# W's first two chunks in halves, proj's first part ahead of them on the same queue, a constant for the constant passes, and m_0's first j copied alone

## The chip, the cores and the metric

The kernel runs on one core of a Trainium2 chip. Its time is the device time of one execution in microseconds (us). Before the change the median of three executions is 317.30 us (317.02 to 317.35).

A core has a matrix engine (TensorE, in the profile PE, with its weight loads as PEld), a vector engine (DVE), a scalar engine (ACT), GpSimd (POOL), and a sync engine (SP) that issues most transfers here. Every engine takes its instructions in order and waits on semaphores for the others. SP, ACT and POOL each have a queue of transfers; all queues are served by the same 16 DMA engines.

## What is computed

Eight sequences x of 512 tokens by 2048 features pass through a conditioning layer with a LoRA adapter per sequence, then through a feed-forward of eight low-rank experts of which each token takes one, and the result is added to x. Cut to what matters:

```python
# conditioning: W (2048 x 2048), one adapter (A, Bm) of rank 16 per sequence
y = einsum('bti,oi->bto', x, W) + b
y = y + einsum('btr,bro->bto', einsum('bti,bir->btr', x, A), Bm) * 2.0
# experts: 8 of rank 16, the best one per token
logits = einsum('bsd,ed->bse', y, route_w)
route_weight = one_hot(argmax(logits)) * max(logits)
h  = einsum('bsd,erd->bser', y, A_ffn)
out = einsum('bser,eor->bso', route_weight[..., None] * h, Bw)
return x + out
```

Everything is float32.

## The kernel before

y is never built. Its only use is a projection on 136 columns: 8 experts x 16 ranks and 8 router rows, side by side in `proj` (2048 x 136). So the kernel folds first: c = W^T proj, a 2048 x 136 matrix, and for each sequence b a matrix m_b = c + the adapter's part. Then each tile of 128 tokens needs only x m_b (the "heads"), the choice of an expert, and one product with `fb`, the experts' second factors (the "deltas"), which is added to x.

**Stage 1, folding (0 to about 70 us).** W comes in 16 chunks of 128 output rows, `w_0` to `w_15`, each a tile of 128 x 2048 (1 MB), six buffers in turn (`load_w`, L104). `pj` is proj as a tile of 128 x 16 x 136, loaded in parts: `load_pj(c0, c1)` (L99) brings the parts c0 to c1 - 1. For chunk oc, `fold_w` (L286) makes 16 matmuls, one for each j (128 of W's columns): the stationary operand is `w_oc[:, j]`, the moving one `pj[:, oc]` of 136 columns, and the result adds up in PSUM over all 16 chunks. A float32 matmul takes two passes of PE, each a weight load and a pass. The results of the 16 j lie in six PSUM banks: `bank_js` (L210) puts j 0 to 2 in bank 0, 4 to 6 in bank 1, 8 to 10 in bank 2, 12 to 14 in bank 3, 3 and 7 in bank 4, 11 and 15 in bank 5, and `fold_w` goes through the banks in the order 0, 1, 4, 2, 3, 5. So its first eight matmuls are j 0 to 7, which read the first 1024 columns of the chunk.

`chunk_w(oc)` (L272) stands ahead of each chunk. It lets ACT and DVE copy one element per partition of the chunk into `paced`, so that both wait until the chunk has landed, and then has SP issue the chunk four further on.

**The start.** The order in the program is: DVE fills `warm`, a 128 x 128 tile, with ones. ACT issues pj's part 0. SP issues w_0, w_1, pj's parts 3 and 4, w_2, pj's parts 5 to 7, w_3. ACT makes one small copy (which loads its function table) and then issues pj's parts 1 and 2. PE multiplies `warm` by `warm` 11 times (22 passes, L136) into a PSUM tile that nobody reads, and then waits for w_0 and pj's part 0. `warm` is used once more, much later, in `project_bias` (L320).

**The end of stage 1.** After the last chunk, ACT copies the six banks to SBUF as c (L299), and `first_products` (L356) adds the adapter's part of sequence 0 to the same banks: 16 small matmuls, j by j over the banks. Then the six banks are copied to SBUF as m_0, alternately by DVE (banks 0, 2, 4) and ACT (banks 1, 3, 5) (L367). `place` finds where a bank's j lie in m_0.

**Stage 2, tokens (about 71.5 us to the end).** 32 tiles of 128 tokens. `heads(t, ...)` (L478) multiplies the transposed tile xT_t with m_b: 16 matmuls (j 0 to 15, in this order), in two halves. DVE routes, PE multiplies with `fb` (`delta`, L628), DVE adds to x (`add_delta`, L650), SP stores. ACT and POOL move 32-row blocks of x into `xq` and DVE transposes them into xT (`shuffle`, `turn_x`). The order of all this is written out by hand; nothing is reordered by a scheduler. x comes in units of two tiles through five buffers, of which the last two take memory that W's tiles and pj gave up.

**Transfers and their counters.** A transfer issued by SP or ACT signals its landing on one of eight counters, taken in turn over the program. An issue that takes a counter whose former transfer is not known to have landed waits for that.

Of the kernel before, what the change touches and what calls it, by code (L numbers as in the profile page):

```python
# [18 lines left out]
def kernel(  # L19
# [32 lines left out]
    nc = tc.nc  # L52
    P = 128
    Q = 32
    NQ = P // Q
    B, T, D = x.shape
# [32 lines left out]
    warm = const.tile([P, P], F32, name="warm")  # L89
# [9 lines left out]
    def load_pj(c0, c1, eng=nc.sync):  # L99
        eng.dma_start(out=pj[:, c0:c1, :], in_=proj_v[:, c0:c1, :])  # L100

    w_tiles = []

    def load_w(oc):  # L104
        wt = wpool.tile([P, D], F32, tag="w", bufs=6, name=f"w_{oc}")
        nc.sync.dma_start(out=wt, in_=w[ts(oc, P), :])
        w_tiles.append(wt)

    load_pj(0, 1, nc.scalar)
    load_w(0)  # L110
    load_w(1)
    load_pj(3, 5)
    load_w(2)
    load_pj(5, 8)
    load_w(3)
# [14 lines left out]
    make_identity(nc, ident)  # L130

    nc.scalar.copy(warm_a[:, 1:2], warm_a[:, :1])
    load_pj(1, 3, nc.scalar)
    pm = ps_s.tile([P, P], F32, tag="s", name="pm")
    for _ in range(11):
        nc.tensor.matmul(pm, warm, warm, start=True, stop=True)  # L136

    own_i = const.tile([P, B], I32, name="own_i")
    nc.gpsimd.iota(own_i, pattern=[[-R, B]], base=0, channel_multiplier=1)
# [62 lines left out]
    parts = (JC, NJ - JC)  # L202

    def at(j):
        q, n = divmod(j, NQ)
        return (1, q) if n == 3 else (0, 3 * q + n)
# [3 lines left out]
    bank_js = {}  # L210
# [5 lines left out]
    ms = {0: [const.tile([P, n, NP], F32, name=f"m0_{n}") for n in parts]}  # L216
# [51 lines left out]
    pcs = [ps_c.tile([P, GRP, NP], F32, name=f"pc_{z}") for z in range(len(bank_js))]  # L268

    paced = const.tile([P, 2], F32, name="paced")  # L270

    def chunk_w(oc):  # L272


        nc.scalar.copy(paced[:, :1], w_tiles[oc][:, :1])  # L275
        nc.vector.tensor_copy(paced[:, 1:], w_tiles[oc][:, :1])  # L276
        if oc + 4 < NO:
            if oc in (2, 3):
                load_pj(4 * oc, 4 * oc + 4)
            load_w(oc + 4)  # L280

    def place(m, js):
        part, n = at(js[0])
        return m[part][:, ds(n, len(js)), :]
# [60 lines left out]
    def adapter_product(b, out, q, n, start=True):  # L345
        nc.tensor.matmul(  # L346
            out,
            ad_q[ts(q, Q), b // 2, n, :],
            g4[ts(q, Q), b, :],
            start=start,  # L350
            stop=True,
            skip_group_check=not start,
            tile_position=(q * Q, 0),
        )

    def first_products():  # L356


        for n in range(3):
            for q in range(NQ):  # L360
                adapter_product(0, pcs[q][:, n, :], q, n, start=False)
        for n in range(2):
            for k in range(2):
                adapter_product(0, pcs[NQ + k][:, n, :], k * HQ, 3 + n, start=False)
        for z in range(NQ + 2):
            js = bank_js[z]
            (nc.scalar.copy if z % 2 else nc.vector.tensor_copy)(  # L367
                place(ms[0], js), pcs[z][:, : len(js), :]
            )

    chunk_w(0)
    for oc in range(NO):
        if oc + 1 < NO:
            chunk_w(oc + 1)
# [42 lines left out]
        if oc == 14:  # L417
            for h in range(2):
                turn_x(0, h)
    first_products()  # L420
    wctx.close()
    ps_o = ctx.enter_context(tc.tile_pool(name="ps_o", bufs=2, space=bass.MemoryType.PSUM))
# [275 lines left out]
    for n in range(2 * NT + LAG + 1):  # L698
# [31 lines left out]
        for q, r in due.get(n - 2, ()):  # L730
            u, k = divmod(q, TPU)
# [50 lines left out]
```

## Time and profile before

The profiled execution took 316.97 us; its span, from the first instruction to the last, is 315.2 us, so 1.8 us lie around it.

| | before |
|---|---|
| median of three executions | 317.30 us (317.02 to 317.35) |
| profiled execution, and its span | 316.97 us, 315.2 us |
| constant passes (L136): first, count, ns of one | 1.06 us, 22, 421 |
| real passes of the folding (L290): first, count, ns of one | 6.38 us, 512, 279 |
| transfer of w_0, w_1, w_2: landing (issue) | 6.15 (0.75), 8.9 (1.2), 12.1 (2.1) us |
| pj's part 0, parts 1 and 2 (ACT's queue): landing (issue) | 6.34 (0.75), 9.35 (1.25) us |
| m_0 copies: ACT, DVE | 70.86 to 72.05, 70.89 to 72.31 us |
| heads: first pass | 71.53 us |

How to read it: a row of the timeline gives the start of a group of instructions in us from the span's start, its length, the engine (SPq and ACTq are the issuing of transfers on SP and ACT), the line of the kernel, the operation, the tile written and the tile read, how many, and in square brackets how long the engine was idle before it and what released it. The chain of waits follows the work that ended last back to the start, at each step to what released it. [...]passes overlap: what counts for the time is the distance from start to start.

### The profile page before, as it was taken

How to read it: one execution, taken by the hardware profiler on the slowest of the kernel's cores; microseconds unless marked ns; L12 is line 12 of the kernel's file. 1: busy time of each engine (PE TensorE's matmuls, PEld its weight loads, DVE VectorE, ACT ScalarE, POOL GpSimd, SP SyncE). 2: the span in 40 equal slices, each digit the busy share in tenths (PEclk: the TensorE clock that was granted, in tenths of full speed). 3: DMA queues.
4: the chain of work that ended last, by engine and by line, in shares of the span. 5: the costliest groups of instructions: out<-in, count | busy, mean ns of one | idle time of the engine just before them, and what ended most of it. 6: DMA issues, size and time to landing. Idle time of an engine off the chain costs nothing.

```text
span 315.2 us, 5653 instructions
## 1 busy us (share of the span) xinstructions
PE 309.1 (98%) x2114; PEld 245.0 (78%) x2114; DVE 230.2 (73%) x390; ACT 189.5 (60%) x311; POOL 187.4 (59%) x284
## 2 busy tenths in 40 slices
PE   8999999999999999999999999999999999999994
PEld 7999999999777877777777768677767777777741
DVE  1010595937999798677988787888788887979684
ACT  2000133738799399559949983998499669912110
POOL 1011083979997866429884975698388929722220
PEclk9999999999999999999999999999999999999998
DMA  7999999989333957784877694848676876253467
GB/s 282 408 361 413 420 419 420 418 338 390 147 135 133 312 222 250 286 286 199 297 289 298 244 384 181 361 164 372 224 309 257 337 295 247 100 234 134 164 243 261
DMA packets 15595, 88.52 MB, mean 281 GB/s; under 512 B 1728, under 2 KB 4048, under 8 KB 5456
## 3 DMA queue, kind: packets, MB, share of 16 engines
q1 hardware_dynamic: 14400, 85.45, 68.9%
q0 software_dynamic: 320, 2.11, 1.6%
q10 hardware_dynamic: 848, 0.61, 0.6%
q8 instruction: 16, 0.26, 0.3%
q14 instruction: 11, 0.09, 0.1%
HBM read 54.60 MB, written 33.55 MB: 280 GB/s over the span
## 4 chain that ended last, share of the span: by engine, by line
PE 96%; DMA 2%; DVE 1%; DVEq 0%; issue 0%
PE ph L482 38%; PE po L648 33%; PE pc L290 19%; DMA pj<-in_proj_dram 2%; PE po L346 2%; PE pg L330 1%; PE ph L648 1%; PE ph L346 1%; PE pe_o L648 1%; DVE x L654 0%; PE pc L346 0%; PE pw L592 0%; DVE m L367 0%; DVEq L778 0%; PE pb L322 0%
## 5 line engine op out<-in xcount | busy, mean ns | idle before, releaser
L253 ACT COPY xq<-x 32x1024 f32<-32x1024 f32 x135 | 140.8, 1043 | 9.6 <-DMA x<-in_x_dram 4.8
L482 PEld LDWEIGHTS ph<-m,xT 128*128 128x128 f32 x1024 | 126.6, 190 | 25.4 <-issue 20.1
L253 POOL COPY xq<-x 32x1024 f32<-32x1024 f32 x121 | 125.5, 1037 | 22.8 <-DMA x<-in_x_dram 6.6
L482 PE MATMUL ph<-m,xT 128*128 128x136 f32 x1024 | 129.7, 280 | 0.3 <-DVE m L367 0.3
L648 PE MATMUL po<-fb,whT 128*128 128x512 f32 x240 | 111.8, 592 | 0.0
L654 DVE TENSOR_TENSOR x<-x,po 128x1024 f32<-128x1024 f32 x60 | 72.5, 1209 | 24.1 <-PE po L648 23.5
L237 DVE STREAM_TRANSPOSE xT<-xq 128x1024 f32<-128x1024 f32 x64 | 78.8, 1235 | 3.8 <-POOL xq L253 3.0
L648 PEld LDWEIGHTS po<-fb,whT 128*128 128x128 f32 x240 | 41.6, 190 | 31.6 <-issue 30.9
L290 PE MATMUL pc<-pj,w 128*128 128x136 f32 x512 | 59.9, 279 | 0.3 <-DMA pj<-in_proj_dram 0.3
L290 PEld LDWEIGHTS pc<-pj,w 128*128 128x128 f32 x512 | 59.5, 190 | 0.6 <-DMA pj<-in_proj_dram 0.6
L610 POOL COPY wq<-wh 32x64 f32<-32x64 f32 (+1 forms) x117 | 26.4, 226 | 54.0 <-DVE wh L534 40.9
L610 ACT COPY wq<-wh 32x64 f32<-32x64 f32 (+1 forms) x91 | 21.6, 238 | 21.3 <-DVE wh L503 10.0
L275 ACT COPY paced<-w 128x1 f32<-128x1 f32 x16 | 3.1, 191 | 39.7 <-DMA w<-in_w_dram 39.7
L276 DVE COPY paced<-w 128x1 f32<-128x1 f32 x16 | 2.4, 151 | 30.7 <-DMA w<-in_w_dram 30.6
L567 ACT COPY m<-ph 128x136 f32<-128x136 f32 x24 | 4.9, 284 | 26.7 <-PE ph L346 22.6
L578 POOL TENSOR_TENSOR m<-m,c 128x408 f32<-128x408 f32 x14 | 14.4, 1052 | 1.6 <-ACT m L573 1.1
L224 POOL COPY ad_q<-ad_ar 32x512 f32<-32x512 f32 x12 | 8.0, 668 | 10.0 <-DMA ad_ar<-in_cond_a_dram,arow_i 9.5
L388 POOL DMA_DIRECT2D bias_o<-in_bias_dram x1 | 0.7, 737 | 17.9 <-DVE bias_o L387 17.9
L571 DVE TENSOR_TENSOR m<-c,po 128x408 f32<-128x408 f32 x14 | 7.5, 576 | 4.0 <-PE po L346 3.9
L579 POOL TENSOR_TENSOR m<-m,c 128x544 f32<-128x544 f32 x7 | 9.4, 1343 | 0.0
L338 DVE TENSOR_TENSOR g<-pg,half 32x272 f32<-32x272 f32 x16 | 7.0, 437 | 3.2 <-PE pg L330 2.9
L615 DVE STREAM_TRANSPOSE whT<-wq 128x256 f32<-128x256 f32 (+1 forms) x13 | 5.2, 404 | 2.7 <-ACT wq L610 2.7
(81 smaller groups left out, 144.4 us busy)
## 6 DMA issues: line engine op xcount, KB each, us to landing
x<-in_x_dram SPq DMA_DIRECT2D x32, 1024.0 KB, 7.9
out_dram<-x SPq DMA_DIRECT2D x28, 1024.0 KB, 4.3
w<-in_w_dram SPq DMA_DIRECT2D x16, 1024.0 KB, 14.3
out_dram<-x SPq DMA_DIRECT2D x4, 512.0 KB, 2.6
out_dram<-x SPq DMA_DIRECT2D x6, 256.0 KB, 3.1
fb<-in_ffn_b_dram SPq DMA_DIRECT2D x1, 1024.0 KB, 17.5
pj<-in_proj_dram SPq DMA_DIRECT2D x2, 272.0 KB, 13.2
out_dram<-x ACTq DMA_DIRECT2D x1, 256.0 KB
```

The lines of the kernel that those rows point to most:

```text
L224: copy(dst[:, :NQ], src[:, ts(q, NQ)])
L237: nc.vector.transpose(dst[:, ts(h, HJ), :].rearrange("p j (g t) -> p g j t", t=Q), src.rearrange("p g (j a) -> p g j a", a=Q)[:, :, ts(h, ...
L253: copy(xq_tiles[u][ts(i, Q), :, g, :].rearrange("p k (j a) -> p k j a", a=Q), src[:, :, :, i, :],)
L290: nc.tensor.matmul(pcs[z][:, n, :], w_tiles[oc][:, ts(j, P)], pj[:, oc, :], start=(oc == 0 and n == 0), stop=(oc == NO - 1), skip_group_ch ...
L346: nc.tensor.matmul(out, ad_q[ts(q, Q), b // 2, n, :], g4[ts(q, Q), b, :], start=start, stop=True, skip_group_check=not start, tile_positio ...
L482: nc.tensor.matmul(ph, xT_tiles[t][:, j, :], place(m, (j,))[:, 0, :], start=(j == 0), stop=(j == NJ - 1),)
L571: nc.vector.tensor_tensor(place(m, js), place(cs, js), banks[q], ALU.add)
L578: nc.gpsimd.tensor_tensor(place(m, js), place(m, js), place(cs, js), ALU.add)
L579: nc.gpsimd.tensor_tensor(m[1], m[1], cs[1], ALU.add)
L610: copy(wq[ts(i, Q), :, ts(q, Q)], wh[ts(q, Q), :, ts(i, Q)])
L648: nc.tensor.matmul(part, whT_tiles[t], fb[:, cols], start=True, stop=True)
L654: nc.vector.tensor_tensor(xs, xs, part, ALU.add)
```

## The change

- `load_w` can bring a chunk in several transfers; w_0 and w_1 come in two of 1024 columns each, into the same tile.
- pj's part 0 is issued by SP, ahead of w_0, and not by ACT.
- ACT issues pj's parts 1 and 2 as two transfers.
- The 11 matmuls ahead of the first chunk read `ones`, a view of the one-column constant 1.0 that the framework writes before the kernel starts, repeated over 128 columns; not `warm`.
- `chunk_w` reads the last column of the chunk in the place of the first.
- m_0 is copied in seven pieces, not six: DVE takes j 0, ACT takes j 1 and 2 of bank 0, and then DVE bank 1, ACT bank 2, DVE bank 3, ACT bank 4, DVE bank 5.

```diff
-    def load_w(oc):
+    def load_w(oc, parts=1):
         wt = wpool.tile([P, D], F32, tag="w", bufs=6, name=f"w_{oc}")
-        nc.sync.dma_start(out=wt, in_=w[ts(oc, P), :])
+        for k in range(parts):
+            cols = ts(k, D // parts)
+            nc.sync.dma_start(out=wt[:, cols], in_=w[ts(oc, P), cols])
         w_tiles.append(wt)
 
-    load_pj(0, 1, nc.scalar)
-    load_w(0)
-    load_w(1)
+
+    load_pj(0, 1)
+    load_w(0, 2)
+    load_w(1, 2)
     load_pj(3, 5)
     load_w(2)
     load_pj(5, 8)
...
     nc.scalar.copy(warm_a[:, 1:2], warm_a[:, :1])
-    load_pj(1, 3, nc.scalar)
+    load_pj(1, 2, nc.scalar)
+    load_pj(2, 3, nc.scalar)
+    ones = nc.const_aps.tensor(1.0, [P, P])
     pm = ps_s.tile([P, P], F32, tag="s", name="pm")
     for _ in range(11):
-        nc.tensor.matmul(pm, warm, warm, start=True, stop=True)
+        nc.tensor.matmul(pm, ones, ones, start=True, stop=True)
...
-        nc.scalar.copy(paced[:, :1], w_tiles[oc][:, :1])
-        nc.vector.tensor_copy(paced[:, 1:], w_tiles[oc][:, :1])
+        nc.scalar.copy(paced[:, :1], w_tiles[oc][:, D - 1 :])
+        nc.vector.tensor_copy(paced[:, 1:], w_tiles[oc][:, D - 1 :])
...
-        for z in range(NQ + 2):
-            js = bank_js[z]
-            (nc.scalar.copy if z % 2 else nc.vector.tensor_copy)(
-                place(ms[0], js), pcs[z][:, : len(js), :]
-            )
+
+        copies = (nc.vector.tensor_copy, nc.scalar.copy)
+        cuts = ((0, 0, 1), (0, 1, 2), *((z, 0, len(bank_js[z])) for z in range(1, NQ + 2)))
+        for k, (z, n0, n) in enumerate(cuts):
+            js = bank_js[z][n0 : n0 + n]
+            copies[k % 2](place(ms[0], js), pcs[z][:, ds(n0, n), :])
```

## The prediction

> **What bounds the kernel now.** I read the page's busy shares first, then the chain that ended last, then the first 20 us of the timeline and the stretch around 71 us, where the chain leaves TensorE.
>
> ```profile
> PE 309.1 (98%) x2114; PEld 245.0 (78%) x2114; DVE 230.2 (73%) x390; ACT 189.5 (60%) x311; POOL 187.4 (59%) x284
> ```
>
> TensorE (PE) works 309.1 of 315.2 us, so an edit pays only where PE does not work, or works on nothing useful. The list of what PE waited for has three entries: 1.1 us for `warm` at the start, 0.3 us for `pj` at 6.38 us, 0.3 us for m_0 at 71.5 us. The change touches all three. The chain of waits, cut to its first 20 us:
>
> ```profile
> 0.75 5.59 DMA pj<-in_proj_dram
> 6.34 0.04 issue
> 6.38 13.70 PE pc L290 x116
> ```
>
> The chain begins with proj's first part: 5.59 us from issue to landing for 68 KB. From 6.38 us PE works without a break. The timeline of the same stretch shows what else stood there (start, length, engine and line):
>
> ```profile
> 0.75 0.41 ACTq L100 DMA_DIRECT2D pj<-in_proj_dram  x1
> 0.75 0.86 SPq L106 DMA_DIRECT2D w<-in_w_dram  x2
> 0.85 0.17 DVE L90 MEMSET warm<- 128x128 f32 x1 [0.85 <-PEq L767]
> 1.06 5.06 PE L136 MATMUL pm<-warm 128*128 128x128 f32 x22 [1.06 <-DVE warm_a L92]
> 6.19 0.19 ACT L275 COPY paced<-w 128x1 f32<-128x1 f32 x1 [3.52 <-DMA w<-in_w_dram]
> 8.99 0.19 ACT L275 COPY paced<-w 128x1 f32<-128x1 f32 x1 [2.61 <-DMA w<-in_w_dram]
> 12.17 0.19 ACT L275 COPY paced<-w 128x1 f32<-128x1 f32 x1 [2.98 <-DMA w<-in_w_dram]
> ```
>
> Three things end within 0.3 us of each other: the 22 constant passes (6.12), w_0 (6.15, seen by its `paced` copy at 6.19) and pj's first part (6.34). Moving one gains little; the change moves all three. What then ends last decides.
>
> **Part 1, constant passes.** They lose their wait for the memset of `warm` (0.85 to 1.02 us) and read a constant that POOL writes at 0.28 us, before the start barrier. SP and ACT issue at 0.75, DVE's first instruction runs at 0.85; I put PE's first pass at 0.85, 0.21 before its 1.06 (ends: 0.75 to 1.06). All 22 passes last 421 ns (the first 579) and start 0.213 us apart: (5.70 - 1.06 - 0.158) / 21. A real pass with 136 columns lasts 279 ns and starts 0.116 us after the last (44.75 us for 384 in the chain). So the constant passes run at half the rate per column, and the first real one at 6.38 at the full rate; the granted-clock row reads 1.00 throughout and does not show this switch. PE could take a real pass 0.213 us after the last constant pass started: 5.91 now, **5.70** changed.
>
> **Part 2, W and proj.** SP now issues pj (68 KB) first, then w_0 in two halves. One issue takes 0.41 to 0.43 us in the timeline, so w_0's first half is issued at 1.18, not 0.75. In the DMA view cut to 0 to 7 us the first bytes move at 1.8 us; about 0.21 MB have moved by 3.0, and from there 400 GB/s. w_0 and pj together (1.12 MB) have then moved at 3.0 + 0.91/0.40 = 5.3; w_0 lands at 6.15, so 0.87 us lie between last byte and landing. Changed, what must move until w_0's first half is in: pj 0.07, the half 0.52, and up to 0.07 of the proj part that ACT now issues beside it: 0.66 MB, at 3.0 + 0.45/0.40 = 4.1, plus 0.3 for the later issue, plus 0.87 = **5.3 us** (4.9 without the later issue; 5.75 with all of it and 4 KB rows a tenth slower and a slower start). pj, first in its queue, lands well before. So the passes end last, at 5.70, and the first real pass comes 6.38 - 5.70 = 0.68 us earlier.
>
> Here a rule of the Trainium skill speaks against the change: *DMA: Bandwidth & Descriptors*, "Rules for kernel authors", wants 128 partitions and at least 1 MiB per DMA, because (section "Anatomy of one DMA", a fit for the GpSimd path) each pays about 2.0 us besides bytes/436 GB/s. Paid one after the other, an estimate from that page makes 3.2 us of each half, and w_0 whole only at 1.18 + 6.4 = 7.6, with w_1 whole at 14.0. The rows deny that such costs add in a filled queue: w_1 landed 2.8 us after w_0, with 136 KB of pj between, which is 1.19 MB at 0.42 MB/us. I take the rows; the fixed part is paid once.
>
> What is late next? One chunk is 32 passes, 3.73 us. The second half of w_0 is read from 5.70 + 16 x 0.116 = 7.6; it lands near 6.7. Chunk 1 starts at 9.43: w_1 landed at 8.95 and lands perhaps 0.4 later whole, but only its first half (near 8.0) is asked for, and pj's part 1 is now a transfer of its own of 68 KB instead of 136 KB that landed at 9.35. Chunk 2 starts at 13.16; w_2 landed at 12.13, with 0.4 it is 12.5. Chunk 3 starts at 16.9, w_3 landed at 15.2. Later chunks have 2 us and more (w_8 34.1 against 36.2). `chunk_w` reads the last column, so ACT's and DVE's pacing copies wait for the whole tile as before; behind them stand only small works that nothing needs before chunk 12. Two more transfers on SP also shift the eight DMA counters: w_2's issue now waits for pj's first part to land (about 3.5), the parts 5 to 7 of pj for w_0's first half, w_3 for pj's part 1 (under 7). The queue holds bytes until about 10.6 at that time, so no engine runs dry; I cost these waits at nothing, and if w_3's issue came only at 11 its landing at 15.2 would slip towards its need at 16.9. At W's end the earlier start is kept: xT_0 is ready at 67.5 for heads at 71.5, g4 at 62.3 for 69.8, xT_2's first half at 79.8 for 81.2. After that loads follow stores, and PE hides both. At most 1.4 us pass through.
>
> **Part 3, first j of m_0.** The timeline around 71 us:
>
> ```profile
> 70.86 1.19 ACT L367 COPY m<-pc 128x408 f32<-128x408 f32 x3 [0.54 <-PE pc L346]
> 70.89 1.42 DVE L367 COPY m<-pc 128x408 f32<-128x408 f32 x3 [3.42 <-PE pc L346]
> 71.53 6.90 PE L482 MATMUL ph<-m,xT 128*128 128x136 f32 x56 [0.27 <-DVE m L367]
> ```
>
> ```profile
>   DVE m L367: 0.7, 2
> ```
>
> The last line is from the heads' line (L482) alone, 71.4 to 76 us: idle before it, in us, and how often. There are two waits for m, not one: 71.53 for j 0, and, pass by pass, a gap from 72.2 to 72.37 for j 3, which lies in bank 4, DVE's third copy (to 72.31). Changed, DVE copies j 0 alone: 0.28 us (ACT needs 273 to 278 ns for such a tile at L567, DVE 300 at L323), done at 71.18, and j 0 starts at 71.23, 0.3 earlier. But in the built order ACT's copy of j 1 and 2 waits for DVE's copy, since both read one bank; so ACT starts at 71.22, not 70.86, and does 272, 408 and 272 columns: 403 + 499 + 403 ns less two overlaps of 0.108 = 1.09, to **72.31**. Bank 4 is now ACT's last. j 3 starts at 72.37 either way: the gain goes into the second wait. I cost part 3 at 0 (ends -0.1 and +0.1 us). DVE and ACT are free 0.2 to 0.3 us later; xT_1 is then ready at 73.6 for its need at 75.4.
>
> **The sum, and the clock.** PE's early real passes may still be slow. *TensorE: Matmul & The Clock Gate* (Part 1) says the array runs at half clock until a busy window of about 3.4 us has passed, and that the window runs free of the kernel's start. The trace agrees as to size (half rate for at least 4.9 us, full rate at 6.38), and puts this execution's switch between 5.91 and 6.38. By the row: passes from 5.70 to the switch cost half that stretch, 0.10 to 0.34, so 0.68 - 0.22 = **0.46 us** is gained. By the rule the switch falls anywhere from 4.5 to 7.9: a late one leaves 0.34, an early one shortens the constant passes too, and then the data at 5.3 sets the start (up to 1.1). I take the row for the middle, the rule for the range. Profiled execution: 316.97 (span 315.2 and 1.8 around it) - 0.46 + 0 = **316.5 us**. The median shown, 317.30, lies 0.33 above that execution; whether the clock's switch makes that spread no run here shows.
>
> **Rivals.**
> *A. Early switch* (0.25): the passes end before 5.5 and W's half decides; 0.75 to 1.2 gained, 316.0. For it: the page's free window. Against: this execution switched late.
> *B. The half lands late* (0.12): at 6.2 instead of 5.3, because the start of the queue is slow (94 to 240 GB/s until 2.8 us); under 0.2 gained, 316.8 to 317.0.
> *C. Slower, by chunk 2* (0.08): 4 KB rows move slower than 8 KB rows, w_2 lands after 13.16 and PE stands. Price: w_0 and w_1 are 2.1 MB, 5.1 us at 410 GB/s; w_2 at 12.5 has 0.66 to spare, so loss begins at 13% slower, and it outweighs the 0.68 from 26% on. At 40% it would be 317.7. No load of 4 KB rows is in this trace; stores with such rows landed in 2.6 us, which tells little of a filled queue.
> *D. The constant does not do it* (0.05): a read that stays on one column is slower than 0.213 us a pass. From 14% on nothing is left; at twice, the start is at 10.4 and the time 321.
> The forecast has 0.50, with its own span 316.2 to 316.7.
>
> **Numbers.** 0.2% is 0.63 us, about what a measurement tells from none. The bound of faster lies that far below the median of before it is timed against: 316.67 by the one shown, 316.35 if that median came out like the profiled execution. Of the forecast's 0.50 I count 0.31 below it; with A's 0.24 that makes 0.55 faster; the rest of the forecast, B and the mild end of C make 0.35; slower keeps 0.10. The range 316.0 to 317.2 holds the forecast, most of A and B.
>
> **What would show it.** First constant pass near 0.85; first real pass at 5.6 to 5.8 with nothing between; some of the first real passes 0.23 apart; `paced` for w_0 after the first real pass; ph's first pass about 0.3 after j 0's product and a longer gap before the seventh; 98% PE as now. Wrong: a gap after the constant passes (B), a gap at chunk 2 or 3 (C), passes over 0.22 apart (D), or ph without its second gap.

## The result, and the profile after

The change makes the kernel slower: 317.82 us in the median of 17 executions (316.96 to 319.34) against 316.93 for the kernel before, timed beside it (316.60 to 317.35, 17 executions). The ratio is 1.0036, 95% interval 1.0025 to 1.0047 (here and below it is not the ratio of the two medians, which would be 1.0028). The forecast was 316.5 us, with a range of 316.0 to 317.2. The spread also grew, from 0.75 to 2.4 us.

| | before | after |
|---|---|---|
| profiled execution, and its span | 316.97, 315.2 us | 317.52, 315.8 us |
| constant passes: first, end | 1.06, 6.12 us | 0.79, 4.81 us |
| first real pass | 6.38 us | 6.44 us |
| w_0, w_1, w_2 landed whole (by ACT's pacing copy) | 6.19, 8.99, 12.17 us | 8.18, 10.83, 13.77 us |
| moved by the DMA engines, 3.0 to 6.5 us | 1.46 MB | 0.90 MB |
| heads: first pass | 71.53 us | 71.27 us |
| GpSimd's first copy of x_1 | 66.75 us | 67.66 us |
| t 3: first heads pass on the chain | 87.85 us | 88.52 us |

The chain of waits after the change, its first 20 us (start, length, what):

```profile
0.75 0.38 SPq L100
1.13 0.06 issue
1.19 5.11 DMA w<-in_w_dram
6.31 0.14 issue
6.44 13.56 PE pc L295 x115
```

The chain begins with SP's issue of proj's part 0 and goes on with w_0's first half, issued behind it: 5.11 us from issue to landing for half the bytes that took 5.4 us whole. The timeline of the stretch:

```profile
0.75 0.38 SPq L100 DMA_DIRECT2D pj<-in_proj_dram  x1
0.79 4.02 PE L141 MATMUL pm<-const-float32-1.0 128*128 128x128 f32 x22 [0.79 <-PEq L773]
1.19 2.03 SPq L108 DMA_DIRECT2D w<-in_w_dram  x4
6.44 13.79 PE L295 MATMUL pc<-pj,w 128*128 128x136 f32 x117 [1.63 <-DMA w<-in_w_dram]
8.18 0.19 ACT L280 COPY paced<-w 128x1 f32<-128x1 f32 x1 [5.94 <-DMA w<-in_w_dram]
10.83 0.19 ACT L280 COPY paced<-w 128x1 f32<-128x1 f32 x1 [2.46 <-DMA w<-in_w_dram]
13.77 0.19 ACT L280 COPY paced<-w 128x1 f32<-128x1 f32 x1 [2.75 <-DMA w<-in_w_dram]
```

The constant passes begin where they should. They end at 4.81, because in this execution the clock switched early, near 3.5 us (passes of 421 ns before, of 273 ns from there on). PE then stands 1.63 us: the bracket of the first real pass names W. The start is 0.06 us later than before. W's first eight chunks land 1.6 to 2.0 us later, the others 0.8 to 1.1 us.

Yet the adapter's products behind the folding begin where they began before (69.85 against 69.83). The 0.6 us are lost later. The chain from 78 to 91 us was PE alone before the change, with these two pieces at the place in question:

```profile
87.16 0.69 PE po L346 x24
87.85 2.05 PE ph L482 x16
```

After the change:

```profile
79.48 2.37 DVE xT L242 x2
...
84.03 1.21 DVE x L660
85.24 1.16 DVE xT L242
86.39 1.12 DVE x L660
87.51 0.04 issue
87.56 0.96 PE po L351 x20
88.52 2.05 PE ph L488 x16
```

Read it from the bottom: the heads of tile 3 come 0.67 us later than before, because `fold_adapter` (L351) needs PSUM that DVE's add (L660) frees; DVE is late since xT_2 is late; and xT_2 waited for GpSimd, which had waited for x_1. GpSimd's copies of x_1, before and after:

```profile
66.75 23.70 POOL L253 COPY xq<-x 32x1024 f32<-32x1024 f32 x22 [1.69 <-DMA x<-in_x_dram]
67.66 23.65 POOL L258 COPY xq<-x 32x1024 f32<-32x1024 f32 x22 [1.87 <-DMA x<-in_x_dram]
```

From there to xT_2 it is 11.85 us before and 11.82 after, so x_1's lateness passes through whole. The chain itself takes another way back, over a short wait of GpSimd at 74.83 us to DVE's m_0 copies (L375, 71.62); taken alone it would accuse those (theory M below).

From 8 to 63 us the page's row has the DMA engines at 90% or more and at about 410 GB/s on average, both times. That bytes not moved in the first 6.5 us therefore arrive later all the way down to x_1 is argued here; the experiments show how far it holds.

### The profile page after: what moved, and what is told of

It is laid out like the page before. It is cut to its first block, busy times and chain, and to the rows that moved or that the text cites. A ratio compares the mean times of both kernels' runs of the same rounds, so it can differ in the third digit from the quotient of the medians.

```text
span 315.8 us, 5660 instructions
## 1 busy us (share of the span) xinstructions
PE 308.8 (98%) x2114; PEld 244.4 (77%) x2114; DVE 230.2 (73%) x391; ACT 189.4 (60%) x311; POOL 186.9 (59%) x284
## 2 busy tenths in 40 slices
DMA packets 15899, 88.52 MB, mean 280 GB/s; under 512 B 1776, under 2 KB 4096, under 8 KB 6016
## 4 chain that ended last, share of the span: by engine, by line
PE 91%; DVE 4%; DMA 2%; POOL 1%; issue 0%; SPq 0%; DVEq 0%; POOLq 0%
PE ph L488 34%; PE po L654 32%; PE pc L295 19%; DVE xT L242 2%; PE po L351 2%; DMA w<-in_w_dram 2%; POOL xq L258 1%; PE pg L335 1%; PE ph L654 1%; DVE x L660 1%; PE ph L351 1%; PE pe_o L654 1%; DVE m L375 0%; PE pc L351 0%; DVE rw L507 0%
## 5 line engine op out<-in xcount | busy, mean ns | idle before, releaser
L258 ACT COPY xq<-x 32x1024 f32<-32x1024 f32 x135 | 140.8, 1043 | 10.9 <-DMA x<-in_x_dram 6.9
L660 DVE TENSOR_TENSOR x<-x,po 128x1024 f32<-128x1024 f32 x60 | 72.5, 1209 | 24.1 <-PE po L654 23.7
```

What stands on the lines that cost most here:

```text
L258: copy(xq_tiles[u][ts(i, Q), :, g, :].rearrange("p k (j a) -> p k j a", a=Q), src[:, :, :, i, :],)
L660: nc.vector.tensor_tensor(xs, xs, part, ALU.add)
```

## The experiments

Each was timed beside the kernel before, whose median was 316.78 to 316.84 us in all of them. **T** is the theory that the new transfers make the queue's start slower and that this is paid at x_1; **M** that the seven copies of m_0 are at fault. Where two kernels were not timed together, their ratios to the kernel before are compared.

### Which part: transfers, or the rest

e1 keeps only the transfers and the pacing column of the change; e2 keeps only the constant and the m_0 copies:

```diff
 e1, against after
-        nc.tensor.matmul(pm, ones, ones, start=True, stop=True)
+        nc.tensor.matmul(pm, warm, warm, start=True, stop=True)
...
 e2, against after
-    load_pj(0, 1)
-    load_w(0, 2)
-    load_w(1, 2)
+    load_pj(0, 1, nc.scalar)
+    load_w(0)
+    load_w(1)
...
-    load_pj(1, 2, nc.scalar)
-    load_pj(2, 3, nc.scalar)
+    load_pj(1, 3, nc.scalar)
```

> Only the transfers' part of the change: w_0 and w_1 in halves, proj's part 0 first on SP, parts 1 and 2 apart on ACT, pacing by the last column; constant passes and m_0 copies as before. Theory T (the queue's start moves fewer bytes, all of W and then x_1 land later, and DVE reaches its add before fold_adapter too late): slower than before by as much as the whole change, 0.5 to 1.3 us, x_1's first xq copy on GpSimd at 67.3 us or later (before 66.75), first real pass at 6.2 to 6.6. Rival M (the seven copies of m_0 hold up DVE and ACT and so xT_2): within 0.2 us of before.

> The change without its transfers: constant passes on the constant and seven m_0 copies stay, W whole, proj's part 0 and parts 1 and 2 on ACT as before. Theory T: within 0.2 us of before; x_1's first xq copy near 66.75, first real pass at 6.3 to 6.4 (the transfers still set it). Rival M: slower than before by 0.5 to 1 us, with PE waiting for DVE's add near 87 us as after the change.

e1: 317.51 us, ratio 1.0021 (1.0011 to 1.0030). e2: 316.83 us, ratio 0.9998 (0.9990 to 1.0006). The transfers are at fault; M falls as a cause of its own. e1's ratio lies below the change's 1.0036; the intervals overlap, so whether transfers and the rest cost more together stays open.

The profiled execution of e1 was its slowest, 319.33 us, and its first real pass came only at 7.09 us (outside what was expected). It shows a second cost. The folding matmuls of e1 at 9.3 to 9.9 us and at 10.2 to 10.9 us (minimum, median and longest of one pass in ns), and its chain:

```profile
L294 PE MATMUL pc<-pj,w x4: 434/434/434, 9.3 to 9.9; 128*128 128x136 f32 x4
```

```profile
L294 PE MATMUL pc<-pj,w x6: 279/280/434, 10.2 to 10.9; 128*128 128x136 f32 x6
```

```profile
7.09 46.40 PE pc L294 x384
```

The last pass of 434 ns starts at 10.2 us: the real passes ran at half rate until about 10.4 us, and 384 of them took 46.40 us, not 44.75. PE had stood 0.96 us before them. So the idle stretch may hold the clock low for another 3.3 us (theory **K**).

### The halves, and x_1

```diff
 e3, against after
-    load_w(0, 2)
-    load_w(1, 2)
+    load_w(0)
+    load_w(1)
...
 e4, against after
-            nc.sync.dma_start(out=fb, in_=ffn_b)
             load_x(1)
+            nc.sync.dma_start(out=fb, in_=ffn_b)
             load_x(2)
```

> The change with w_0 and w_1 in one transfer each; proj's part 0 stays first on SP, parts 1 and 2 stay apart on ACT. If the halves (4 KB rows) slow the queue's start (T-halves): at least 0.4 us faster than the change, w_0 whole at 6.3 to 6.7 instead of 8.1, x_1's xq copy near 66.8. If the order of proj's parts does it (T-proj): within 0.3 us of the change, w_0 whole at 7.5 or later.

> The change as it is, with x_1's two transfers issued ahead of fb's. Theory T: the start is as after the change (w_0 whole near 8 us), but x_1 lands 2 us or more earlier, PE no longer waits for DVE near 87 us, and the time is 0.4 to 1.2 us below the change, so within 0.3 us of before. If the loss does not go through x_1's landing: within 0.2 us of the change.

e3: 317.36 us, ratio 1.0030 (1.0014 to 1.0046). w_0 is whole at 6.2 us and 1.32 MB move from 3 to 6.5 us, so behind part 0 the halves do slow the queue. But the time hardly follows: e3 is still 0.57 us above before, and its interval covers the change's 1.0036. Its chunks land no later than before (the last one is copied from at 58.63 us, before at 59.24), yet GpSimd begins x_1 at 67.13, 0.38 us later than before. Why, no run here shows; so T is not the whole account. Three of its twelve executions took 319.1 to 319.2 us.

e4: 317.14 us, ratio 1.0021 (1.0009 to 1.0032). The start is the change's (w_0 whole at 8.05 us), x_1 no longer stops GpSimd, and PE does not wait near 87 us. Against the kernel before, the loss falls from 0.89 to 0.35 us; by the ratios it falls by 0.0015 of 0.0036. The intervals overlap, but e9 and e10 below differ by the same edit: 1.12 to 0.82 us, and 0.0015 again. So x_1's late landing was a good part of the loss, 0.3 to 0.5 us, and not all of it.

### The clock

```diff
 e9 and e10, against after (e10 with x_1 ahead of fb as well)
-    for _ in range(11):
+    for _ in range(13):
...
 e11, against before
-    for _ in range(11):
+    for _ in range(8):
```

> The change with 13 constant matmuls, not 11, so that PE works until the data is there (26 slow passes end near 6.4 us). Theory K (the idle stretch between the constant passes and the first real pass, 0.6 to 1.6 us after the change, can keep the clock low or lower it again, which costs up to 1.7 us in some executions): the spread shrinks, no execution above 318.2 us, the median falls from 317.8 to 317.2 to 317.5; what is left is x_1's late landing. If the slow executions come from the transfers alone: executions above 318.5 stay in about a quarter of the runs.

> The change with 13 constant matmuls and x_1's transfers ahead of fb's: both suspected costs away. If clock and x_1 are all there is: 316.6 to 317.0 us, within 0.15 us of before, no execution above 317.6. If a third cost exists: 0.3 us or more above before.

> The kernel before with 8 constant matmuls, not 11: the constant passes end near 4.7 us, 1.6 us before the first real pass; transfers untouched. Theory K: 0.3 to 1 us slower than before in the median, some executions 1.5 to 2 us above the fastest, in these the first real passes 0.23 us apart. If the idle stretch does not matter for the clock: within 0.1 us of before, spread as before (0.7 us).

e9 is a miss: 317.90 us (316.99 to 319.35), ratio 1.0038 (1.0027 to 1.0048), no better than the change in median or spread. e10 comes out on the side of a third cost, 317.60 us, ratio 1.0023 (1.0016 to 1.0029), though none of its 21 executions exceeds 318.25. e11's median, 316.77, is that of before, which contradicts what was expected of it; but its fourteen executions fall in two groups, ten from 316.59 to 317.02 and four from 318.29 to 318.85, and nothing lies between. The kernel before has no such second group in 63 executions. The transfers of e11 are those of before, so fewer constant passes, and with them 1.5 us without work ahead of the first real pass, do cost 1.5 to 2.1 us in some executions. That the cause there is the clock was seen in e1's profile only; none of e11's four was profiled. K fits such a group and does not explain the even spread of the change.

Once the clock had switched, a pause of that length did no harm. After the change and in e16 (below) the constant passes were already at 273 ns when PE stopped, PE stood 1.6 and 1.7 us, and from the second real pass on each lasted 279 ns. So K would concern only executions in which the switch is still to come.

e10's profile shows a third cost. Its chain:

```profile
4.13 9.92 DMA w<-in_w_dram
14.06 0.04 issue
14.10 5.94 PE pc L295 x49
```

w_2 landed at 14.06 us, after chunk 2's turn, and PE waited inside the folding. In the change's own profile w_2 was there at 13.77, for a chunk 2 due at 6.44 + 2 x 3.73 = 13.90: 0.13 us to spare. In e10 the wait is 0.24 us (13.74 to 14.10 between two passes that elsewhere start 0.116 apart). How much of the change's spread comes from there, and how much from the clock, the runs do not split.

### proj's place

```diff
 e6, against after
-    load_pj(0, 1)
+    load_pj(0, 1, nc.scalar)
...
-    load_pj(1, 2, nc.scalar)
-    load_pj(2, 3, nc.scalar)
+    load_pj(1, 3, nc.scalar)
```

e12 makes only the second of these edits, e13 only the first.

> The change with proj's part 0 back on ACT and parts 1 and 2 in one transfer there; w_0 and w_1 stay in halves. If the place and number of proj's transfers slow the start: first real pass at 6.0 to 6.3 us, w_0 whole at 6.3 to 7, x_1's xq copy at 66.9 or earlier, 0.4 us or more below the change. If the halves do it: w_0 whole near 8 us as after the change and the time within 0.3 us of the change.

> The change with proj's parts 1 and 2 in one transfer on ACT again; part 0 stays first on SP, chunks in halves. If part 0's place ahead of w_0 costs the start: like the change, 317.5 us or more, w_0 whole near 8 us. If the splitting of parts 1 and 2 does: like the kernel with both undone, near 316.5 us, w_0 whole near 6.8 us.

> The change with part 0 back on ACT, parts 1 and 2 still apart behind it; chunks in halves. The other half of the same question: if part 0's place costs the start, near 316.5 us, first real pass near 5.7 us; if the splitting does, 317.3 us or more.

| | us, median (span of executions) | ratio to before (95%) | first real pass | w_0 whole |
|---|---|---|---|---|
| e6, both undone | 316.51 (316.22 to 316.92) | 0.9989 (0.9982 to 0.9996) | 5.62 us | 6.8 us |
| e12, parts 1 and 2 together | 317.49 (317.19 to 319.22) | 1.0037 (1.0019 to 1.0055) | 6.66 us | 7.8 us |
| e13, part 0 back on ACT | 316.42 (316.22 to 316.86) | 0.9986 (0.9978 to 0.9995) | 5.51 us | 6.8 us |

The place of part 0 is the cause. With that one argument put back, the change is slightly faster than the kernel before, and PE starts about where the prediction put it (5.70 us). It makes the loss with whole chunks as well: proj on ACT with whole chunks is e2 (0.9998), with halves e6 (0.9989); part 0 on SP with whole chunks is e3 (1.0030), with halves the change (1.0036); parts 1 and 2 together or apart make no difference in e12 and e13. So the halves alone did no harm. And x_1 goes with it: in the eight kernels with a small transfer on SP ahead of some part of W and x_1 behind `fb` (the change, e1, e3, e9, e12 and, below, e16 to e18), GpSimd begins x_1 at 66.94 to 67.75 us; with nothing ahead of W on SP (before, e2, e6, e11, e13, e15) at 66.21 to 66.75.

The waits of PE in e13, and its timeline:

```profile
PE pm L141 <- PEq L773: 0.8, 1, 0.8
PE pc L295 <- DMA pj<-in_proj_dram: 0.2, 1, 0.2
```

```profile
5.51 14.75 PE L295 MATMUL pc<-pj,w 128*128 128x136 f32 x125 [0.20 <-DMA pj<-in_proj_dram]
6.82 0.19 ACT L280 COPY paced<-w 128x1 f32<-128x1 f32 x1 [4.14 <-DMA w<-in_w_dram]
```

PE waits 0.2 us, where the change waits 1.6. The start that the prediction describes is e6's: its clock switched late, its constant passes end at 5.82, its first real pass is at 5.62.

### What about its place

Three kernels asked why. e16 leaves proj on ACT and has SP issue a 4 KB transfer, the adapters' ids, ahead of w_0; e17 has SP issue part 0 between w_0's halves; e18 takes all proj from ACT.

```diff
 e16, against e13
+    nc.sync.dma_start(out=it_i, in_=itok.to_broadcast([P, B]))
     load_w(0, 2)
...
 e17, against after
-    load_pj(0, 1)
...
+            if oc == 0 and k == 0:
+                load_pj(0, 1)
...
 e18, against after
     load_w(0, 2)
+    load_pj(1, 3)
     load_w(1, 2)
...
-    load_pj(1, 2, nc.scalar)
-    load_pj(2, 3, nc.scalar)
```

> proj's part 0 back on ACT ahead of parts 1 and 2; in its place ahead of w_0 SP issues the adapters' ids (4 KB in 128 rows of 32 bytes), which ACT issued after chunk 1. If a transfer ahead of W on SP costs by delaying W's issue (0.44 us): w_0's first half issued at 1.19 and landed at 5.7 or later, 316.8 us or more. If it is part 0's own place (its bytes, or ACT's queue without it): first real pass at 5.8 or earlier, 316.3 to 316.6 us.

> The change with part 0 on SP between w_0's first and second half: W's first half is issued at 0.75 again. If the delay of W's issue is what costs: first real pass near 5.6 to 5.9, 316.3 to 316.7 us. If part 0's rows on SP's ring, or ACT's parts 1 and 2 beside W's first half, slow the queue: w_0 whole at 7.5 us or later, 317.2 us or more.

> The change with parts 1 and 2 in one transfer on SP between w_0 and w_1; ACT issues no proj at all. If ACT's parts beside W's first half are what slows the queue in the change: 1.15 MB or more moved from 3 to 6.5 us (the change 0.90), first real pass at 5.9 or earlier, 316.4 to 316.8. If not: 0.9 to 1.0 MB, first real pass at 6.2 or later, 317.2 or more.

e16: 317.61 us, ratio 1.0017 (1.0008 to 1.0026); w_0's first half is issued at 1.19 and lands at 6.8 us, although the transfer ahead of it is 4 KB. e17: 317.05 us, 1.0013 (1.0003 to 1.0023); the half, issued at 0.75, is in by 5.5 us, but part 0 now lands at 6.0 and w_0 whole at 7.8. e18: 317.37 us, 1.0017 (1.0008 to 1.0027); 1.04 MB from 3 to 6.5 us, first real pass at 6.36: ACT's transfers beside W are not the main cost, though all three lose less than the change.

So it is not part 0's bytes. In these kernels a transfer of many small rows (32 bytes in e16, 544 in the others) ahead of a 4 KB-row part of W on SP costs W its place in line and slows what follows. How, the DMA view shows best in a stretch of one microsecond, 3 to 4 us (packets, MB, share of the 16 engines' time; q1 is SP's queue, q10 ACT's). Before:

```profile
q1 hardware_dynamic: 48, 0.39, 94.4%
q10 hardware_dynamic: 48, 0.03, 10.3%
```

After, 3 to 4 us, 4 to 5 us, and then 6 to 7 us:

```profile
q1 hardware_dynamic: 51, 0.21, 97.6%
```

```profile
q1 hardware_dynamic: 58, 0.22, 86.8%
```

```profile
q1 hardware_dynamic: 101, 0.38, 94.0%
```

A packet is one row: 8 KB before (0.39 MB in 48), 4 KB in the halves (0.21 MB in 51). From 3 to 4 us a 4 KB row took an engine as long, on average, as an 8 KB row: 16 x 0.976 / 51 = 0.31 us after, 16 x 0.944 / 48 = 0.31 us before. So half the bytes move with the engines just as taken up. From 6 to 7 us it is 16 x 0.94 / 101 = 0.15 us, half of that. The 8 KB rows of before show no such change: SP's queue moves 48 of them from 6 to 7 us too. In e13 the rate rises two microseconds earlier (51 packets from 3 to 4 us, 91 from 4 to 5). Why 4 KB rows are slow at first, and what ends it, no run here shows.

### The rest

```diff
 e14, against e6
-            nc.sync.dma_start(out=fb, in_=ffn_b)
             load_x(1)
+            nc.sync.dma_start(out=fb, in_=ffn_b)
...
 e15, against e6
-        nc.tensor.matmul(pm, ones, ones, start=True, stop=True)
+        nc.tensor.matmul(pm, warm, warm, start=True, stop=True)
```

e15 has the six m_0 copies of before as well.

> Halves and constant passes of the change, proj's parts on ACT as before, and x_1's transfers ahead of fb's. If x_1's landing holds back what the earlier start gained (x_1 lands no earlier than before, PE starts 0.6 us earlier): 0.1 to 0.3 us below the kernel without the x_1 move, 316.2 to 316.4. If not: the same, 316.5.

> The kernel before with w_0 and w_1 in halves and nothing else: passes on warm, six copies of m_0, proj on ACT. The first real pass then waits for the constant passes, which start 0.27 us later: 5.9 us; 316.6 to 316.8 us, 0.1 to 0.3 above the kernel that also has the constant and the seven copies. If the constant gives nothing: 316.5.

e14: 316.51 us, ratio 0.9985 (0.9976 to 0.9993), the same as e6: with proj on ACT, x_1 is in time (GpSimd begins it at 66.29 us in e6). e15: 316.72 us, ratio 0.9993 (0.9984 to 1.0002), first real pass at 5.92. That is 0.2 us above e6, as the constant's earlier start should give; the intervals overlap. The lowest median is that of e13, the change with one argument put back; e6 and e14 cannot be told from it.

## Why the prediction was wrong

**The step that failed is one term of part 2:** "the half 0.52, and up to 0.07 of the proj part that ACT now issues beside it: 0.66 MB, at 3.0 + 0.45/0.40 = 4.1". The 0.40 MB/us was read from 8 KB rows and used for 4 KB rows behind a transfer of small rows. After the change 0.21 and 0.23 MB moved in the two microseconds from 3 to 5. With 0.22 MB/us the term is 3.0 + 0.45/0.22 = 5.0, and with the 0.3 and the 0.87 of the prediction the half lands at 6.2 instead of 5.3; measured were 6.30. So this term is nearly the whole error of the start, and it turns the 0.68 us that PE was to gain there into a loss of 0.06.

**The later issue of W was put at 0.3 us, without a reason,** though the prediction itself has W issued 0.43 us later. In e16 a 4 KB transfer ahead of W takes the issue from 0.75 to 1.19 us, and the half lands 1.3 us later than in e13. That is the later issue and the slower queue together.

**A term that is missing: a later x_1.** Of the slack named for stage 2, "xT_2's first half at 79.8 for 81.2", 1.4 us, was not the first to go. `fold_adapter` behind two adds of DVE had 0.4 us (before, DVE's add ended at 86.6 and L346's passes into po began at 86.98), and the add came 0.9 us later. The prediction asked what an earlier PE could lose there; it did not ask what later data would cost. e4 and e10 put that at 0.3 to 0.5 us. The rest of the loss (0.35 us in e4) was not taken apart: the clock and w_2 have a part in it, of unknown size.

**"What is late next"** was too hopeful by the same rate: w_0's second half near 6.7 and w_2 at 12.5, measured 8.2 and 13.8.

**Rivals.** B (the half lands late) came true as to the half, at a chance of 0.12, but not in its price: it still had a gain of up to 0.2. C (4 KB rows are slower), at 0.08, came true in its cause. w_2 came 1.3 us later than put, a quarter of the 5.1 us for two chunks, so the first of its two marks (13%) was passed and the second (26%) just about reached; but since PE began at 6.44 and not at 5.70, chunk 2 was not late in the profiled execution, only in e10's. The load that cost was the one C did not name, x_1. A's early switch came too (3.5 us, outside the 4.5 to 7.9 that the prediction took from the rule), and won nothing, since the data was not there. D did not come: the constant is read at 0.213 us a pass like `warm`.

**Rule against row.** The Trainium skill's rule (*DMA: Bandwidth & Descriptors*, "Rules for kernel authors": at least 1 MiB per DMA) was set aside because a filled queue does not pay the fixed cost each time. For w_1 that holds: 2.65 us from w_0 whole to w_1 whole, in 4 KB rows, where the prediction's estimate from that page had 6.4. For the first half it does not: 5.11 us from issue to landing, where the estimate had 3.2. Nor does the time settle it for the rule: with part 0 ahead on SP the intervals do not tell whole chunks from halves (e3 1.0030, the change 1.0036), and with proj on ACT the halves come out no slower (e6 0.9989, e2 0.9998).

**What was right.** The constant passes (first at 0.79, put at 0.85). Part 3 at nothing: the first heads pass was put at 71.23 and ran at 71.27, the second wait was to end at 72.37 and PE's weight load resumes at 72.38, and e2 came out at 0.9998. These are times on the clock of the kernel before, and the folding happened to end where it ended there. The clock as a risk for early passes: in e6 the first 384 real passes begin 0.76 us earlier than before and end only 0.2 us earlier (at 50.93 for 51.13), so 0.56 us went there, more than the 0.22 allowed for. But it was counted only as passes made slow by being early, and not as an idle stretch that can leave the clock low afterwards, as in e1's profile (1.65 us). The 0.46 us of the whole sum belong to a start that the change does not have; the kernels that have it gain 0.27 (e6) and 0.37 us (e13). That their times, 316.5 and 316.4, lie so near the forecast 316.5 is luck in part, because the kernel before, timed beside them, had 316.8 and not the 316.97 that the sum started from.

## What to carry to other kernels

Issue first, on the queue that everything waits for, the transfer that everything waits for. In these kernels a small transfer ahead of it on the same queue cost far more than its bytes (4 KB in e16), and on the other queue it travelled beside at no cost that shows. A rate taken from a profile holds for the row size and the moment it was read at: check both before using it for a start. Where the DMA queue is full for long, ask of any loss at its head not only which first reader is late, but which last one.

## What was not expected of the hardware

From 3 to 4 us a 4 KB row on SP's queue took an engine as long after the change as an 8 KB row before it (0.31 us), and from 6 to 7 us half of that. The clock's switch, read from the length of the passes, came between 3.5 us (after) and 10.4 us (e1) in kernels whose passes began within 0.3 us of each other, and the granted-clock row of the profile reads 1.00 throughout and shows none of it.
